# Another dealing of an adder layer's taps over three engines, and a first scan unit prepared by halves

## The chip, the cores and the metric

The kernel runs on one core of a Trainium2 chip. The metric is the device time of one execution in microseconds. Engines are named as in the profile: PE is TensorE, DVE is VectorE, ACT is ScalarE, POOL is GpSimd, SP issues the DMAs. PE is given a clock that can be throttled; the profile shows the share that was granted.

## The reference, cut to what matters

The program has four layers: an adder convolution, a Mamba block with three scan branches and a fusion, an attention with routed experts, and a deep linear-attention and spectral part. The change touches the first and the start of the second. After a group normalization of the input, with `x` as (8, 128, 16, 16), the first layer is

```python
def adder2d(x, W, stride, padding):           # W is (128, 128, 3, 3)
    ...
    out = -jnp.abs(W_col[:, :, None] - X_col[None, :, :]).sum(1)
```

Each of 128 filters takes nine taps of 128 channels, and sums the absolute differences over channels and taps. The result is added to `x`. The second layer normalizes over channels, projects to 256 channels `u`, and for each of the branches f, b and s does

```python
uc = jax.nn.silu(causal_conv1d(u, cw, cb))    # four taps
proj = uc @ xw.T                              # dt, Bm, Cm
delta = jax.nn.softplus(dt @ dw.T + db)
return selective_scan(uc, delta, -jnp.exp(A_log), Bm, Cm, D)
```

The scan has 16 states: h = exp(delta A) h + (delta u) B, and y sums h C over the states and adds u D.

## The kernel before

All data is fp32. Channels lie on the 128 partitions.

The first layer (`adder_layer`, L304) holds three copies of the padded image, shifted by 0, 1 and 2 columns; `tap(k)` is a view of one of them, 128 x 2048 (8 images of 256 pixels). Filters go in NG = 4 groups of FG = 32. For each filter and tap one engine makes a 128 x 2048 tile `d`, and PE adds it up over the channels (`add`, four matmuls of 512 columns with a selector of 32 columns, each on its own quarter of the columns of the array), all into one PSUM tile `o` of the group.

- Taps 1, 3, 5 (and 7, in some filters) are an absolute value on ACT (L421), with tiles of the tag da.
- Taps 0, 2, 4, 6, 8 (and 7 in the filters of MORE) are a maximum with the weight on DVE (L419), with tiles of the tag dv. By |w - x| = 2 max(w, x) - w - x, PE adds them with the selector 2, and the sums of weights and inputs are taken off by `wall` and `xsum`; MORE enters both.
- In the filters of JOIN, taps 0 and 2 are joined: the maximum of tap 0 is held, and one fused instruction on DVE (L413) makes max(tap 2, w) + held, in place. PE then has one tap less to add.

The pool of d has four buffers of each tag, so each producer can be four tiles ahead of PE. A planner may put instructions of an engine in another order than they are written in, by priorities; waits on buffers and data are its own. When a group is done, DVE adds `xsum` (L428), four DMAs on SP turn the result into `total` (L430), and DVE makes E.X from x, `wall` and `total`, by blocks of 512 (L434).

`x`, `total`, the shifted copies, the weights and the rest lie in one pool, l0, opened first. The pools of the second layer lie over it, and a tile there waits for the last access to what lay below.

The second layer's scans (`_scans`) treat units of (branch, pair of images), each a block of 512 columns and two halves of 128 channels. `first_unit` prepares the first of them with nothing beside it: centering on PE, square, Ln and Exp on ACT, the projection `pu` of each half, the convolution of each half as four matmuls with diagonal weights (eight passes of 512 columns, fp32 taking two), bias, sigmoid as Exp, Ln, Exp on ACT, the product `uc` on DVE, the projection `pp`, its copy `proj`, the DMA of its rows to DRAM, and softplus. Then `chunk` loads rows of B and C back, broadcast over partitions (bs and cs, two states to a load, SP queue); `decays` makes exp(delta A) in PSUM on ACT; `inputs` makes du x B (on DVE for the first state, on POOL for all others). The scan itself (L825) is on DVE, one per half and state, then the product with C (on POOL for states 1 and 8), then PE sums over the states. That loop is written in a fixed order by hand (`manual_schedule`), with the preparation of later units and the fusion in the gaps of it.

Of the kernel before, what the change touches and what calls it, by code (L numbers as in the profile page):

```python
# [10 lines left out]
F32 = mybir.dt.float32  # L11
AF = mybir.ActivationFunctionType
ALU = mybir.AluOpType
# [3 lines left out]
P = 128  # L17
B = 8
# [280 lines left out]
MORE = tuple(r for r in range(FG) if r % 5 in (0, 2))  # L299
JOINED = (0, 2)  # L300
JOIN = tuple(r for r in range(FG) if r % 5 in (1, 3))


def adder_layer(E):  # L304
# [8 lines left out]
    with ExitStack() as ctx:  # L313
        p = ctx.enter_context(tc.tile_pool(name="l0", bufs=1))
        accp = ctx.enter_context(tc.tile_pool(name="l0acc", bufs=3))
        absp = ctx.enter_context(tc.tile_pool(name="l0abs", bufs=4))
        po = ctx.enter_context(tc.tile_pool(name="l0po", bufs=2, space=PSUM))
        ps = ctx.enter_context(tc.tile_pool(name="l0ps", bufs=2, space=PSUM))

        x = p.tile([P, B, L], F32, tag="x", name="x0")  # L320
# [54 lines left out]
        def tap(k):  # L375
            kh, kw = divmod(k, 3)
            return shifted[kw][:, :, kh * 16 : kh * 16 + L]
# [26 lines left out]
        total = p.tile([P, NBLK, BLK], F32, tag="total", name="total")  # L404
        for g in range(NG):
            out = po.tile([P, BLK], F32, tag="o", name="o")
            for r in range(FG):
                f = g * FG + r
                maxima = MAX_TAPS + (MORE_TAPS if r in MORE else ())
                joined = JOINED if r in JOIN else ()  # L410
                for k in range(9):
                    if k in joined[1:]:
                        nc.vector.scalar_tensor_tensor(held, tap(k), w[:, k, f : f + 1], held, ALU.max, ALU.add)  # L413
                        add(out, sel2[:, FG - 1 - r : 2 * FG - 1 - r], held, False, False)
                        continue
                    d = absp.tile([P, B, L], F32, tag="dv" if k in maxima else "da", name="d")
                    wk = w[:, k, f : f + 1]
                    if k in maxima:
                        nc.vector.tensor_scalar(d, tap(k), wk, None, ALU.max)  # L419
                    else:  # L420
                        nc.scalar.activation(d, tap(k), AF.Abs, scale=-1.0, bias=wk)  # L421
                    if k in joined:
                        held = d
                        continue
                    sel = sel2 if k in maxima else sel1
                    row = slice(FG - 1 - r, 2 * FG - 1 - r)
                    add(out, sel[:, row], d, r == 0 and k == 0, r == FG - 1 and k == 8)
            nc.vector.tensor_add(sums[:, g, :], xsum, out)  # L428
            for i in range(NBLK):
                nc.sync.dma_start(total[g * FG : (g + 1) * FG, i, :], sums[i * FG : (i + 1) * FG, g, :])  # L430
# [71 lines left out]
def _scans(E, ctx, F):  # L502
# [116 lines left out]
    def softplus(k, s, h, proj, d, e, r, tag, gen):  # L619
# [7 lines left out]
        nc.scalar.activation(d, pd, AF.Relu, bias=db)  # L627
        yield LATER
        nc.scalar.activation(e, e, AF.Exp, scale=-1.0)
        one_e = ps.tile([P, UT], F32, tag=tag, name="one_e")  # L630
        nc.scalar.activation(one_e, e, AF.Identity, bias=E.ones[:, 0:1])
        yield LATER
        nc.vector.scalar_tensor_tensor(e, one_e, -1.0, e, ALU.add, ALU.subtract)
        nc.scalar.activation(r, one_e, AF.Ln)
        gen.tensor_sub(r, r, e)
# [10 lines left out]
    def prepare(k, s, p, got):  # L646
# [16 lines left out]
        for h in range(2):  # L663
            yield from softplus(k, s, h, proj, delta[:, h, :], pre[:, h, :], sig[:, h, :], "s", nc.gpsimd)
# [3 lines left out]
    def first_unit(k, s, p, got):  # L668
# [13 lines left out]
        us[p] = two.tile([P, 2, UT], F32, tag="u", name="u1")  # L682
        tags = ("f", "s")
        for h in range(2):
            pu = ps.tile([P, UT], F32, tag=tags[h], name="pu")
            E.mm(pu, E.w["in_proj"][:, h * P : (h + 1) * P], t)
            (nc.vector.tensor_copy if h else nc.scalar.copy)(us[p][:, h, :], pu)
# [5 lines left out]
        new, pre, sig, proj = tiles()  # L693
        uc, delta = new["uc"], new["delta"]
        for h in range(2):
            pc = ps.tile([P, UB, L], F32, tag=tags[h], name="pconv")
            for _ in convolution(k, s, h, us[p], pc):
                pass
            biased(s, h, pc, pre[:, h, :])
            for _ in sigmoid(sig[:, h, :], pre[:, h, :]):  # L700
                pass
            nc.vector.tensor_mul(uc[:, h, :], pre[:, h, :], sig[:, h, :])
        nc.scalar.copy(proj, projections(k, uc, proj, "f"))
        nc.sync.dma_start(new["rows"], proj[DTR:, :])
        parts = [
            softplus(k, s, h, proj, delta[:, h, :], pre[:, h, :], sig[:, h, :], tags[h], nc.vector) for h in range(2)
        ]
        for part in parts:
            next(part)
        for part in parts:  # L710
            for _ in part:
                pass
        nc.vector.tensor_mul(new["du"], delta, uc)  # L713
        got.update(new)
# [21 lines left out]
    def inputs(r, gen=nc.gpsimd):  # L736
        if r < states:
            dbs[r] = three.tile([P, 2, UT], F32, tag="db", name="dbu")
            gen.tensor_tensor(dbs[r], got[r // NST]["du"], bc(row("bs", r), 1, 2), ALU.mult)  # L739
# [52 lines left out]
    first_unit(*units[0], got[0])  # L792
# [3 lines left out]
    for g in range(3):  # L796
        decays(g)
    inputs(0, nc.vector)
# [1033 lines left out]
```

## Time and profile before

| | us |
|---|---|
| runs | 3077.44 median of 3, 3069.77 to 3080.7 |
| profiled execution, its own time | 3075.62 |
| its span | 3073.8 |
| PE busy | 2875.2 (94%) |
| DVE busy | 2451.8 (80%) |
| ACT busy | 2216.1 (72%) |
| first layer's taps on PE | 33.65 to 984.2 |
| last block of E.X done | 989.7 |
| first scan starts | 1023.64 |
| mean granted clock of PE | 0.988 |

A group's line gives the source line, engine and operation, the tiles written and read, the shape and the count; then the busy time and the mean duration of one in ns; then how long the engine was idle just before these instructions, and what ended the wait. A line of the timeline begins with the start and the length in us, and merges equal neighbours (xcount). A line of a window gives each engine's busy time in it, the granted clock, the share of the DMA engines and GB/s. PE's matmuls all have the line of a helper, L279, so their tiles tell them apart.

### The profile page before, as it was taken

Reading aid. Unit: us, or ns where it says so; the run is one execution under the profiler, and the core shown is the slowest. Engines: PE = TensorE matmul, PEld = TensorE weight load, DVE = VectorE, ACT = ScalarE, POOL = GpSimd, SP = SyncE. Lnnn points to the kernel's source line nnn. Section 1 sums busy time; section 2 is a strip of 40 time slices with the busy share of each in tenths; the row PEclk is TensorE's granted clock in tenths of the full one; section 3 lists DMA queues with packets and bytes.
Section 4 is the critical chain, followed back from the end, with each engine's and each line's share of the span. In section 5 each row is a group of like instructions: output and inputs, shape, how many; then the busy total and the mean of one; then the engine's idle time right before and its main releaser. Section 6 shows DMA issues by size and latency. Waiting matters only on the chain.

```text
span 3073.8 us, 42374 instructions
## 1 busy us (share of the span) xinstructions
PE 2875.2 (94%) x16602; PEld 1283.8 (42%) x16602; DVE 2451.8 (80%) x3452; ACT 2216.1 (72%) x2652; POOL 731.5 (24%) x445
## 2 busy tenths in 40 slices
PE   6999999999998788898898888999999999999999
PEld 2333333333332233443343444555555555654444
DVE  6999999999997799999999627887877777784331
ACT  6999999999997777778777324467778778777111
POOL 3000000000000599998999300000000000000110
PEclk9999999999999999999999999999999999999999
DMA  1000000000000444444344200000000000001100
GB/s 41 1 1 5 1 1 5 1 1 5 1 1 4 155 145 143 140 145 144 133 158 144 71 28 1 13 1 14 14 14 1 13 14 1 14 1 45 48 28 14
DMA packets 39197, 131.53 MB, mean 43 GB/s; under 512 B 7491, under 2 KB 10573, under 8 KB 37589
## 3 DMA queue, kind: packets, MB, share of 16 engines
q1 hardware_dynamic: 38564, 128.02, 11.9%
q8 instruction: 131, 2.15, 0.3%
q10 hardware_dynamic: 432, 0.79, 0.1%
q14 instruction: 70, 0.57, 0.1%
HBM read 125.91 MB, written 1.84 MB: 42 GB/s over the span
## 4 chain that ended last, share of the span: by engine, by line
PE 68%; DVE 16%; ACT 7%; POOL 5%; issue 3%; DMA 1%; DVEq 0%; ACTq 0%; POOLq 0%
PE o L279 31%; PE p L279 8%; DVE st L825 5%; PE acc L279 4%; PE g L279 4%; PE conv L279 3%; POOL dbu L739 2%; PE pc L279 2%; PE var L279 2%; PE pf L279 2%; PE pq L279 2%; PE po L279 1%; PE pn L279 1%; PE pconv L279 1%; PE pa L279 1%
## 5 line engine op out<-in xcount | busy, mean ns | idle before, releaser
L279 PE MATMUL o<-d,sel 128*32 128x512 f32 x8800 | 946.5, 592 | 5.5 <-DVE d L419 5.5
L421 ACT ACTIVATE d<-sh,w 128x2048 f32<-128x2048 f32 x460 | 886.2, 1996 | 64.0 <-PE o L279 54.4
L419 DVE TENSOR_SCALAR d<-sh,w 128x2048 f32<-128x2048 f32 x640 | 789.4, 1291 | 47.7 <-PE o L279 39.6
L739 POOL TENSOR_TENSOR dbu<-du,bs 128x1024 f32<-128x1024 f32 x191 | 446.9, 2365 | 994.8 <-DVE du L713 989.9
L279 PEld LDWEIGHTS o<-d,sel 128*32 128x32 f32 x8800 | 299.1, 110 | 652.1 <-issue 540.6
L825 DVE TENSOR_TENSOR_SCAN st<-da,dbu 128x512 f32<-128x512 f32 x384 | 446.1, 1206 | 17.6 <-POOL dbu L739 14.6
L279 PE MATMUL acc<-st,cst 128*128 128x512 f32 x768 | 369.4, 611 | 60.2 <-DVE st L836 59.9
L752 ACT ACTIVATE da<-delta,neg_a 128x510 f32<-128x510 f32 x384 | 256.9, 684 | 79.5 <-DVE st L825 78.1
L279 PEld LDWEIGHTS acc<-st,cst 128*128 128x128 f32 x768 | 142.2, 193 | 257.3 <-issue 139.5
L836 DVE TENSOR_TENSOR st<-st,pcs 128x1024 f32<-128x1024 f32 x168 | 205.2, 1222 | 17.9 <-ACT da L752 0.5
L1310 POOL TENSOR_TENSOR lw<-lw,turn 128x640 f32<-128x640 f32 x8 | 10.0, 1255 | 717.9 <-DVE turn L1309 626.6
L1087 ACT ACT_TABLE_LOAD x134 | 171.9, 1283 | 2.4
L1764 ACT COPY ug<-p 128x512 f32<-128x512 f32 x64 | 37.5, 585 | 180.4 <-PE p L279 180.4
L744 ACT COPY pcs<-cs 128x512 f32<-128x512 f32 x168 | 97.8, 582 | 55.8 <-DVE st L836 50.6
L279 PE MATMUL conv<-pad,f 128*128 128x512 f32 x288 | 133.1, 596 | 2.8 <-ACT pad L1001 2.3
L279 PE MATMUL p<-un,lw 128*128 128x512 f32 x256 | 123.6, 605 | 3.8 <-DVE un L1381 2.1
L413 DVE SCALAR_TENSOR_TENSOR d<-sh,w,d 128x2048 f32<-128x2048 f32 x52 | 122.3, 2352 | 1.9
L279 PE MATMUL p<-g,lw 128*128 128x512 f32 x256 | 116.4, 597 | 3.9 <-ACT g L1095 3.9
L279 PE MATMUL p<-T,H 128*128 128x512 f32 x256 | 113.8, 596 | 6.3 <-DVE ug L1766 5.3
L279 PE MATMUL g<-ug,me 128*128 128x512 f32 (+1 forms) x320 | 111.9, 509 | 0.0
L1095 ACT ACTIVATE ex<-ex 128x352 f32<-128x352 f32 x128 | 62.4, 494 | 52.2 <-DVE ex L1575 51.0
L279 PE MATMUL pf<-lw,rk 128*128 128x352 f32 x256 | 95.4, 470 | 0.3 <-DVE ek L1525 0.2
(347 smaller groups left out, 3946.2 us busy)
## 6 DMA issues: line engine op xcount, KB each, us to landing
bs<-rows SPq DMA_DIRECT2D x96, 512.0 KB, 3.7
cs<-rows SPq DMA_DIRECT2D x96, 512.0 KB, 4.6
m<-in_Mphi SPq DMA_DIRECT2D x8, 1024.0 KB, 4.8
lw<-in_layers SPq DMA_DIRECT2D x8, 948.0 KB, 4.7
f<-in_fuse SPq DMA_DIRECT2D x2, 1152.0 KB, 7.7
T<-in_T SPq DMA_DIRECT2D x1, 2064.0 KB, 7.8
x<-in_x SPq DMA_DIRECT2D x4, 256.0 KB, 7.1
total<-sums SPq DMA_DIRECT2D x16, 64.0 KB, 2.0
```

The source lines that it names most:

```text
L279: self.nc.tensor.matmul(out, lhsT=lhsT, rhs=rhs, start=start, stop=stop)
L413: nc.vector.scalar_tensor_tensor(held, tap(k), w[:, k, f : f + 1], held, ALU.max, ALU.add)
L419: nc.vector.tensor_scalar(d, tap(k), wk, None, ALU.max)
L421: nc.scalar.activation(d, tap(k), AF.Abs, scale=-1.0, bias=wk)
L739: gen.tensor_tensor(dbs[r], got[r // NST]["du"], bc(row("bs", r), 1, 2), ALU.mult)
L744: nc.scalar.copy(pcs[r], row("cs", r))
L752: nc.scalar.activation(das[g % 3][:, :, 1:], d[:, :, 1:], AF.Exp, scale=a)
L825: nc.vector.tensor_tensor_scan(st[:, h, :], da, dbs[r][:, h, :], 0.0, ALU.mult, ALU.add)
L836: nc.vector.tensor_tensor(st, st, bc(pcs[r][:, :], 1, 2), ALU.mult)
L1087: S.tc.keep_in_program_order(S.nc.scalar.preload_act_table_set(name))
L1095: S.nc.scalar.activation(out, src, func, **kw)
L1764: nc.scalar.copy(dst, p4)
```

## The change

In the first layer MORE is now 10 filters in 32 (r % 10 in 0, 3, 6; 13 before), and all other 22 are joined (13 before). In a joined filter the taps are written in the order 1, 0, 3, 2, 5, 4, 6, 7, 8. `x` and `total` have a pool of their own, opened after the others of the layer.

In `first_unit` both halves are projected first. Half 1's convolution is one scaling and three fused multiply-adds on DVE, straight from the projection in PSUM; its sigmoid is Exp on ACT, +1 and a reciprocal on DVE. Half 0 keeps PE and ACT. The copy of half 1's `u`, and the decay rates `neg_a`, are written behind the DMA of the rows. In softplus, for this unit alone, the Relu, the +1, and the last two sums are on DVE. The scan's first input is made by halves on POOL, and so the loads of bs and cs, the decays and these products stand between the halves.

```diff
-MORE = tuple(r for r in range(FG) if r % 5 in (0, 2))
+MORE = tuple(r for r in range(FG) if r % 10 in (0, 3, 6))
 JOINED = (0, 2)
-JOIN = tuple(r for r in range(FG) if r % 5 in (1, 3))
...
+        last = ctx.enter_context(tc.tile_pool(name="l0last", bufs=1))
...
-        x = p.tile([P, B, L], F32, tag="x", name="x0")
+        x = last.tile([P, B, L], F32, tag="x", name="x0")
...
-        total = p.tile([P, NBLK, BLK], F32, tag="total", name="total")
+        total = last.tile([P, NBLK, BLK], F32, tag="total", name="total")
...
-                joined = JOINED if r in JOIN else ()
-                for k in range(9):
+                joined = () if r in MORE else JOINED
+                order = (1, 0, 3, 2, 5, 4, 6, 7, 8) if joined else range(9)
+                for k in order:
+                    wk = w[:, k, f : f + 1]
                     if k in joined[1:]:
-                        nc.vector.scalar_tensor_tensor(held, tap(k), w[:, k, f : f + 1], held, ALU.max, ALU.add)
-                        add(out, sel2[:, FG - 1 - r : 2 * FG - 1 - r], held, False, False)
-                        continue
...
+                        d = held
+                        nc.vector.scalar_tensor_tensor(d, tap(k), wk, d, ALU.max, ALU.add)
...
@@ softplus
-        nc.scalar.activation(d, pd, AF.Relu, bias=db)
+        if alone:
+            nc.vector.tensor_scalar(d, pd, db, 0.0, ALU.add, ALU.max)
+        else:
+            nc.scalar.activation(d, pd, AF.Relu, bias=db)
         yield LATER
         nc.scalar.activation(e, e, AF.Exp, scale=-1.0)
...
+        if alone:
+            one_e = r
+            nc.vector.tensor_scalar_add(one_e, e, 1.0)
...
@@ first_unit
+        pus = [ps.tile([P, UT], F32, tag=t, name="pu") for t in tags]
         for h in range(2):
...
+            E.mm(pus[h], E.w["in_proj"][:, h * P : (h + 1) * P], t)
+        nc.scalar.copy(us[p][:, 0, :], pus[0])
+
+        u1, p1 = (a.rearrange("p (b l) -> p b l", l=L) for a in (pus[1], pre[:, 1, :]))
+        nc.vector.tensor_scalar(p1, u1, E.v("cw" + s, 7), E.v("cb" + s, 1), ALU.mult, ALU.add)
+        for m in range(1, 4):
+            o = p1[:, :, m:]
+            nc.vector.scalar_tensor_tensor(o, u1[:, :, : L - m], E.v("cw" + s, 7 - m), o, ALU.mult, ALU.add)
+        pc = ps.tile([P, UB, L], F32, tag="f", name="pconv")
+        for _ in convolution(k, s, 0, us[p], pc):
+            pass
+        t = sig[:, 1, :]
+        nc.scalar.activation(t, pre[:, 1, :], AF.Exp, scale=-1.0)
+        nc.vector.tensor_scalar_add(t, t, 1.0)
+        nc.vector.reciprocal(t, t)
+        nc.vector.tensor_mul(uc[:, 1, :], pre[:, 1, :], t)
+        biased(s, 0, pc, pre[:, 0, :])
+        for _ in sigmoid(sig[:, 0, :], pre[:, 0, :]):
+            pass
+        nc.vector.tensor_mul(uc[:, 0, :], pre[:, 0, :], sig[:, 0, :])
+        nc.scalar.copy(proj, projections(k, uc, proj, "f"))
+        nc.sync.dma_start(new["rows"], proj[DTR:, :])
+        got.update(new)
+        yield
+        nc.scalar.copy(us[p][:, 1, :], pus[1])
...
+        for h, part in enumerate(parts):
             for _ in part:
                 pass
-        nc.vector.tensor_mul(new["du"], delta, uc)
-        got.update(new)
+            nc.vector.tensor_mul(new["du"][:, h, :], delta[:, h, :], uc[:, h, :])
+            yield
...
-    first_unit(*units[0], got[0])
+    first = first_unit(*units[0], got[0])
+    next(first)
     for c in range(2):
         chunk("bs", 0, c)
         chunk("cs", NST, c)
-    for g in range(3):
-        decays(g)
-    inputs(0, nc.vector)
+    dbs[0] = three.tile([P, 2, UT], F32, tag="db", name="dbu")
+    for h in range(2):
+        next(first)
+        nc.gpsimd.tensor_mul(dbs[0][:, h, :], got[0]["du"][:, h, :], row("bs", 0))
+        decays(h)
+    decays(2)
     inputs(1)
     rows_of_c(0)
```

The planner's order around it: on DVE the half 0 product `uc` stands before half 1's, behind the reciprocal; PE does both `pp`, then the D term of half 0 (`acc`), then the two `pd` of softplus; the first scan stands on DVE before half 1's last sum and its `du`.

## The prediction, made before the changed kernel had run

> **What bounds the kernel now.** I began with the page's shares and its costliest groups. The first layer's three groups are the largest of their engines, and the fifth line here is its join:
>
> ```profile
> L279 PE MATMUL o<-d,sel 128*32 128x512 f32 x8800 | 946.5, 592 | 5.5 <-DVE d L419 5.5
> L421 ACT ACTIVATE d<-sh,w 128x2048 f32<-128x2048 f32 x460 | 886.2, 1996 | 64.0 <-PE o L279 54.4
> L419 DVE TENSOR_SCALAR d<-sh,w 128x2048 f32<-128x2048 f32 x640 | 789.4, 1291 | 47.7 <-PE o L279 39.6
> ...
> L413 DVE SCALAR_TENSOR_TENSOR d<-sh,w,d 128x2048 f32<-128x2048 f32 x52 | 122.3, 2352 | 1.9
> ```
>
> The idle column says who leads: TensorE waited 5.5 us in all (the start), while ScalarE (54.4) and VectorE (39.6) waited for TensorE to give buffers back. So this third of the span is TensorE's: 1100 taps (8 records each) in 946.5 us, 0.8605 us a tap. The timeline gives the start-to-start intervals, which a mean of durations hides:
>
> ```profile
> 938.37 2.35 DVE L413 SCALAR_TENSOR_TENSOR d<-sh,w,d 128x2048 f32<-128x2048 f32 x1
> ...
> 940.64 10.85 DVE L419 TENSOR_SCALAR d<-sh,w 128x2048 f32<-128x2048 f32 x9
> ...
> 941.40 13.52 ACT L421 ACTIVATE d<-sh,w 128x2048 f32<-128x2048 f32 x7 [1.07 <-PE o L279]
> ...
> 951.64 1.29 DVE L419 TENSOR_SCALAR d<-sh,w 128x2048 f32<-128x2048 f32 x1
> ...
> 952.96 2.35 DVE L413 SCALAR_TENSOR_TENSOR d<-sh,w,d 128x2048 f32<-128x2048 f32 x1
> ```
>
> A maximum follows a maximum after (10.85-1.29)/8 = 1.195 us; the join starts 952.96-951.64 = 1.32 after the maximum that it needs; 940.64-938.37 = 2.27 after a join comes the next. An absolute value takes (13.52-2.00)/6 = 1.92.
>
> Then the timeline between the layers, where one chain runs at a time:
>
> ```profile
> 989.75 0.35 ACT L689 ACTIVATE neg_a<-vecs 128x32 f32<-128x32 f32 x2 [11.22 <-DVE X L434]
> 990.01 0.58 ACT L674 ACTIVATE ln_rstd<-xc 128x512 f32<-128x512 f32 x1
> ...
> 1002.91 0.69 ACT L603 ACTIVATE pre<-pconv,vecs 128x512 f32<-128x512 f32 x1 [4.74 <-PE pconv L279]
> ...
> 1009.12 0.69 DVE L702 TENSOR_TENSOR uc<-pre,sig 128x512 f32<-128x512 f32 x1 [2.72 <-ACT sig L611]
> ...
> 1013.06 0.69 ACT L626 ACTIVATE pre<-pd,vecs 128x512 f32<-128x512 f32 x1 [1.53 <-PE pd L279]
> ...
> 1023.64 2.34 DVE L825 TENSOR_TENSOR_SCAN st<-da,dbu 128x512 f32<-128x512 f32 x2
> ...
> 1027.15 4.56 DVE L825 TENSOR_TENSOR_SCAN st<-da,dbu 128x512 f32<-128x512 f32 x4
> ```
>
> With zero at the start of the xc matmul (987.70), the second half's uc begins at 21.4, softplus at 25.4, the first scan at 35.9 and state 1's at 39.45. From there VectorE repeats with no gap, so a shift of state 1 shifts everything after it.
>
> **Part 1, the dealing.** Per group of 32 filters 22 are joined (13 before) and 10 move tap 7 to VectorE (13). Over 128 filters: joins 52 -> 88, maxima 640 -> 592, absolute values 460 -> 472, taps on TensorE 1100 -> 1064.
> - TensorE: 1064 x 0.8605 = 915.6, 31 us less.
> - ScalarE: 472 x 1.92 = 906.
> - VectorE: 592 x 1.195 + 88 x 2.27 = 707 + 200; in the changed order 52 joins stand right behind the maximum that they need, and pay 1.32-1.195 more: 6.5. Together 914 (the same sum before: 890).
>
> Three nearly equal queues, where TensorE led by 50 us. VectorE's fifth tap starts at 40.79 in the trace (the start before it does not change). From there VectorE has 914 - 4 x 1.195 = 909, three group sums inside at 0.6 (2 us) and the first filter's stalls as now (2 us): done at 953.8. The lag of TensorE behind VectorE's last tap stays 984.19-981.22 = 2.97. That makes 956.8, if VectorE never waits for a buffer. How often does it? In the trace a buffer is usable 1.11 to 1.17 us after its tap's first matmul, and data is used 0.05 us after it is made. I carried the three queues through both orders tap by tap with these intervals and four buffers for each producer. For before this gives ScalarE 53 us of waits and VectorE 39 (trace: 54.4 and 39.6). For after it gives VectorE 6 us of buffer waits and TensorE some 35 short waits of 0.25 us. So 963 instead of 984.2: **-21 us**. With no wait at all it is -27; with the release 0.15 us later, or 15 us of waits, -13.
>
> The tap order (1,0,3,2,...) lets TensorE begin a joined filter with ScalarE's tap; it adds no work. Three memsets fewer on GpSimd at the start lie before its wait for a load: nothing.
>
> **Part 2, x and total in a pool of their own.** neg_a lay over x, so ScalarE waited for the last X (989.72), and the Square behind it in the queue, ready at 988.9, started at 990.01. Now neg_a waits only for the last taps: **-1.1 us**. What is late next is the matmul itself.
>
> **Part 3, halves.** Each step at its trace duration, zero as above.
> - pu starts at 6.7 (now 7.8), its halves are out at 8.7 and 10.4; eight warm passes of convolution for half 0 until 14.05, as the trace has them after the first half.
> - Removed from TensorE: eight passes of 0.43 (3.4 us). Added to VectorE for half 1: one tensor-scalar and three fused steps out of PSUM, 0.69 + 3 x 0.72: done at 13.35. ScalarE Exp 0.63, VectorE +1 0.55 (row L681): 14.6. Then the reciprocal of 128x512, for which there are only small rows:
>
> ```profile
> L361 DVE RECIPROCAL rs<-rs 128x8 f32<-128x8 f32 x1 | 0.2, 203 | 4.4 <-ACT rs L357 4.4
> ...
> L941 DVE RECIPROCAL sm<-sm 128x2 f32<-128x2 f32 x8 | 1.3, 158 | 0.0
> ```
>
> Six elements more cost 45 ns: 7.5 ns each, so 512 cost 3.9 us. The other end is [...]as in the multiply: 0.69. [...]I take 3.9, done at 18.5.
> - Half 0 on ScalarE: bias, copy of u1 (0.5, new in between), Exp, Ln, Exp, so uc 0 could start at 14.05+3.35 = 17.4. It is queued behind the reciprocal: 18.55; uc 1 at 19.2. With 0.69 it would be 17.4, and the sum 1.15 lower.
> - pp 0 starts at 19.3 (the last one at 22.2 now).
>
> Here the clock speaks. TensorE now stays at work beside half 0's sigmoid; afterwards it idles from 14 to 19.3.
>
> ```profile
> 997.00:999.00 2.00, 2.00 (x3) 0.65 (x2) 0.00 (x0) 0.58 (x1) 0.00 (x0) 0.50 0.00 0
> 1001.00:1003.00 2.00, 2.00 (x6) 0.94 (x5) 0.00 (x0) 0.09 (x1) 0.00 (x0) 1.00 0.00 0
> ```
>
> The third figure from the end is the granted clock; at 0.50 passes follow each other after 0.855 us, at 1.00 after 0.43. [...] By the row of now (pp at full clock) the four pp passes end at 21.2 and softplus begins at 22.9. [...]they run at half: pp until 22.95, acc half 0 until 24.4, pd after that[...]: softplus at 25.6, against 25.4 now. [...]
> - Softplus to state 1, by the new order. From its start t: Relu, +1, and the subtractions alternate on VectorE with Exp and Ln on ScalarE; delta 0 at t+5.8, du 0 at 6.5, GpSimd's half product (1.26, row L635's shape) until 7.8, scan 0 of state 0 at 7.85. This is a new wait: behind that scan on VectorE stand the add and the du of half 1, though ready at 7.1, and GpSimd's second product waits for that du. So add and du until 10.4, product until 11.7, scan 11.75, C product until 14.2; GpSimd's state 1 product (2.35, behind both halves in its queue) until 14.1. State 1 scans at t+14.25, against 1027.15-1013.06 = 14.1 now. The first scan comes 2.7 us earlier relative to softplus, and gives it back one state on.
> - On SP the rows store and its four loads keep their order; the first bs goes out 1.7 us after the store, as now, at about t-0.3; GpSimd needs it at t+6.5 and such loads land in about 3.7 (row of issues): hidden, 3 us spare. If late, it costs its lateness once.
>
> State 1: 25.6+14.25 = 39.85 against 39.45: **+0.4 us**. Full clock all along and a short reciprocal: -3.5. Half clock also in the convolution[...]: +2.5.
>
> **Sum.** 3073.8 - 21 + 0.4 = 3053.2 span. Outside the span lie 3075.62-3073.8 = 1.8, and the median shown is 1.8 above the profiled time: **3057**.
>
> **Rivals.**
> 1. The queues hold each other up: 15 to 20 us of buffer waits rather than 6. For: averages within 1.5% on three engines and only four buffers. Against: a joined or unjoined filter costs VectorE the same 7.2 us, so its load doesn't swing. Time: 3066.
> 2. All works: VectorE never waits, TensorE keeps its clock. -27-3 = 3047. Against: the gap of 5 us.
> 3. Slower: ScalarE waits 1.07 us once per joined filter (52 times, all of its 54 us). If that were a price of joining rather than slack, ScalarE would need 906 + 88 x 1.07 = 1000, 56 above TensorE's 944: 3130. It decides from 0.45 us a join. Against: TensorE never waits for ScalarE in the trace.
> 4. The dealing gains nothing: buffer waits of 27 us or more on VectorE: 3077. Against: it waits 39 us now only because TensorE is 50 us longer.
>
> **Numbers.** Likeliest 0.74 (its own range 3049 to 3064); rival 1 0.13; rival 2 0.09; rivals 3 and 4 0.02 each. Runs of before differ by 11 us (3069.8 to 3080.7), and 0.3%, about 9 us, is what tells from no change: below 3068.2. Range 3046 to 3068: from rival 2 to rival 1's middle. Faster 0.91, same 0.07 (rival 4 and the slower part of rival 1), slower 0.02.
>
> **What would show it.** Rows of the layer: VectorE's idle for TensorE under 15 us, TensorE idle near 10 with VectorE named, X some 21 us earlier. neg_a before the Square with no wait for X. Reciprocal near 3.9 us, uc 0 directly behind it. Clock 0.50 at pp. Scan of half 1 about 3.9 us behind half 0's. Wrong would be: ScalarE or TensorE still leading the layer, or a state 1 more than 4 us from its place behind X.

## The result, and the profile after

The changed kernel takes 3056.92 us (median, 3054.22 to 3062.77); the kernel before, beside it, 3076.87. The ratio is 0.9941, with a 95% interval of 0.9928 to 0.9954. The profiled execution took 3055.99 us with a span of 3054.2. The forecast was 3057; that the median meets it to 0.1 us is chance, since single executions lie up to 6 us away from it. One execution in the tables below, of the kernel with 124 units joined, took 3705.6 us at a granted clock of 0.748; it is left out of that kernel's median and ratio.

The first layer's groups on the page after:

```profile
L279 PE MATMUL o<-d,sel 128*32 128x512 f32 x8512 | 922.8, 593 | 7.5 <-DVE d L421 5.5
L423 ACT ACTIVATE d<-sh,w 128x2048 f32<-128x2048 f32 x472 | 899.6, 1994 | 29.8 <-PE o L279 23.2
L421 DVE TENSOR_SCALAR d<-sh,w 128x2048 f32<-128x2048 f32 x592 | 724.3, 1290 | 12.5 <-PE o L279 9.4
...
L417 DVE SCALAR_TENSOR_TENSOR d<-sh,w,d 128x2048 f32<-128x2048 f32 x88 | 206.7, 2349 | 1.9
```

The idle column has changed sides. VectorE waits 9.4 us for buffers where it waited 39.6, ScalarE 23.2 where it waited 54.4. TensorE's busy time fell by 24 us though its taps fell by 31 us' worth: a stretched tap counts as busy. From start to start, 36 of the 1064 taps take more than the usual 0.86 us, 33 of them about 1.07 and three 1.43: 8.6 us that before did not have. Each of the 36 starts 0.05 or 0.06 us after an instruction of VectorE has ended, so it is VectorE's tiles that TensorE waits for. The last tap ends at 962.62 us instead of 984.19.

The timeline of the changed kernel between the layers (start and length in us; brackets hold the idle time before and its releaser):

```profile
959.75 0.35 ACT L724 ACTIVATE neg_a<-vecs 128x32 f32<-128x32 f32 x2 [1.72 <-issue]
...
966.14 2.08 PE L279 MATMUL xc<-X,center 128*128 128x512 f32 x2 [3.52 <-DVE X L436]
...
973.76 3.75 PE L279 MATMUL pu<-xn,w_in_proj 128*128 128x512 f32 x4 [2.79 <-issue]
...
981.87 3.35 DVE L712 RECIPROCAL sig<-sig 128x512 f32<-128x512 f32 x1
...
985.14 0.63 DVE L717 TENSOR_TENSOR uc<-pre,sig 128x512 f32<-128x512 f32 x1
...
985.82 3.43 PE L279 MATMUL pp<-uc,w_xproj 128*40 128x512 f32 x4 [3.97 <-DVE uc L717]
...
991.52 0.69 ACT L628 ACTIVATE pre<-pd,vecs 128x512 f32<-128x512 f32 x1 [1.66 <-PE pd L279]
...
998.07 1.26 POOL L824 TENSOR_TENSOR dbu<-du,bs 128x512 f32<-128x512 f32 x1 [965.56 <-DVE du L737]
...
999.36 1.22 DVE L853 TENSOR_TENSOR_SCAN st<-da,dbu 128x512 f32<-128x512 f32 x1 [1.18 <-POOL dbu L824]
...
1003.27 1.22 DVE L853 TENSOR_TENSOR_SCAN st<-da,dbu 128x512 f32<-128x512 f32 x1 [1.38 <-POOL dbu L824]
...
1005.66 3.44 DVE L853 TENSOR_TENSOR_SCAN st<-da,dbu 128x512 f32<-128x512 f32 x3
```

State 1's first scan, the third scan of the kernel, stands 43.04 us behind the last tap (42.96 before) and 39.52 behind xc (39.45 before). So the shift at state 1 is -21.5 us, all of it from the first layer. From there to the end before took 2046.65 us and after 2048.54: 1.9 us went back, and the span is 19.6 us shorter.

The same stretch by windows (busy time of PE, PEld, DVE, ACT and POOL; the third figure from the end is the granted clock):

```profile
965.60:979.20 13.60, 9.59 (x11) 3.35 (x12) 5.58 (x10) 2.62 (x5) 0.00 (x0) 0.50 0.04 10
979.30:986.00 6.70, 2.73 (x7) 0.93 (x7) 5.93 (x6) 3.67 (x6) 0.00 (x0) 1.00 0.00 0
986.10:989.40 3.30, 3.30 (x5) 0.61 (x4) 0.26 (x1) 0.12 (x1) 0.00 (x0) 0.50 0.00 0
```

The half clock covers xc, var and both pu, ends 1.9 us into the 4.5 us of the convolution, and comes back for pp. In the kernel before it had set in one matmul later: var and pu had the same lengths, but xc ran at the full clock, and so in the forecast.

```profile
987.70 1.12 PE L279 MATMUL xc<-X,center 128*128 128x512 f32 x2 [3.51 <-DVE X L434]
990.64 2.07 PE L279 MATMUL var<-ln_rstd,mean 128*128 128x512 f32 x2 [1.82 <-ACT ln_rstd L674]
995.51 3.75 PE L279 MATMUL pu<-xn,w_in_proj 128*128 128x512 f32 x4 [2.79 <-issue]
```

### The profile page after: what moved, and what is told of

It is laid out like the page before. It is cut to its first block, busy times and chain, and to the rows that moved or that the text cites. A ratio compares the mean times of both kernels' runs of the same rounds, so it can differ in the third digit from the quotient of the medians.

```text
span 3054.2 us, 41648 instructions
## 1 busy us (share of the span) xinstructions
PE 2859.8 (94%) x16306; PEld 1260.9 (41%) x16306; DVE 2469.8 (81%) x3449; ACT 2226.4 (73%) x2658; POOL 733.0 (24%) x444
## 4 chain that ended last, share of the span: by engine, by line
PE 67%; DVE 17%; ACT 7%; POOL 5%; issue 3%; DMA 1%; DVEq 0%; ACTq 0%; POOLq 0%
PE o L279 30%; PE p L279 8%; DVE st L853 5%; PE acc L279 5%; PE g L279 4%; PE conv L279 3%; POOL dbu L763 2%; PE pc L279 2%; PE var L279 2%; PE pf L279 2%; PE pq L279 2%; PE pa L279 1%; PE po L279 1%; PE pn L279 1%; PE px L1610 1%
## 5 line engine op out<-in xcount | busy, mean ns | idle before, releaser
L279 PE MATMUL o<-d,sel 128*32 128x512 f32 x8512 | 922.8, 593 | 7.5 <-DVE d L421 5.5
L423 ACT ACTIVATE d<-sh,w 128x2048 f32<-128x2048 f32 x472 | 899.6, 1994 | 29.8 <-PE o L279 23.2
L421 DVE TENSOR_SCALAR d<-sh,w 128x2048 f32<-128x2048 f32 x592 | 724.3, 1290 | 12.5 <-PE o L279 9.4
L279 PEld LDWEIGHTS o<-d,sel 128*32 128x32 f32 x8512 | 273.9, 110 | 655.6 <-issue 533.6
L279 PE MATMUL acc<-st,cst 128*128 128x512 f32 x768 | 382.2, 631 | 59.0 <-DVE st L864 58.6
L417 DVE SCALAR_TENSOR_TENSOR d<-sh,w,d 128x2048 f32<-128x2048 f32 x88 | 206.7, 2349 | 1.9
```

The costliest lines, as they stand in the source:

```text
L279: self.nc.tensor.matmul(out, lhsT=lhsT, rhs=rhs, start=start, stop=stop)
L417: nc.vector.scalar_tensor_tensor(d, tap(k), wk, d, ALU.max, ALU.add)
```

## The experiments

Each kernel below the second row was run beside the kernel before, in three sets of runs in which before's medians were 3078.20, 3078.01 and 3079.33 us. Rows of different sets are compared by their ratios and by the marks in the trace, not by their medians. "Last tap", "transition" (last tap to the third scan) and "rest" (from there to the end) are from each one's profiled execution.

| kernel | median us | ratio to before, 95% | last tap | transition | rest |
|---|---|---|---|---|---|
| before | 3076.87 | | 984.19 | 42.96 | 2046.65 |
| changed | 3056.92 | 0.9941, 0.9928 to 0.9954 | 962.62 | 43.04 | 2048.54 |
| dealing alone | 3054.04 | 0.9937, 0.9919 to 0.9955 | 962.73 | 43.85 | 2045.12 |
| dealing and pool | 3047.80 | 0.9923, 0.9896 to 0.9950 | 963.93 | 42.12 | 2039.55 |
| pool and halves | 3081.42 | 1.0016, 1.0007 to 1.0025 | 984.69 | 41.96 | 2055.65 |
| taps 0 to 8 | 3092.62 | 1.0063, 1.0043 to 1.0082 | 996.71 | 41.99 | 2045.50 |
| taps 0 to 8, 5 buffers | 3046.02 | 0.9894, 0.9874 to 0.9913 | 951.78 | 41.87 | 2048.55 |
| 5 buffers | 3046.22 | 0.9899, 0.9880 to 0.9919 | 953.05 | 42.93 | 2040.52 |
| 124 units joined | 3094.61 | 1.0063, 1.0041 to 1.0085 | 997.63 | 43.05 | 2049.22 |
| extra matmuls | 3055.44 | 0.9930, 0.9911 to 0.9949 | 962.15 | 37.76 | 2046.59 |
| both halves first | 3058.82 | 0.9944, 0.9924 to 0.9964 | 964.08 | 43.31 | 2044.81 |
| old unit, 5 buffers | 3045.56 | 0.9887, 0.9871 to 0.9904 | 953.30 | 43.08 | 2048.52 |
| extra matmuls, 5 buffers | 3041.23 | 0.9878, 0.9863 to 0.9893 | 952.19 | 37.75 | 2051.86 |
| old unit, extra, 5 buffers | 3043.28 | 0.9885, 0.9871 to 0.9900 | 953.01 | 39.67 | 2051.12 |

### One part at a time

The dealing alone, on the kernel before:

```diff
+MORE = tuple(r for r in range(FG) if r % 10 in (0, 3, 6))
...
+                joined = () if r in MORE else JOINED
+                order = (1, 0, 3, 2, 5, 4, 6, 7, 8) if joined else range(9)
```

> The kernel before with the new dealing of the first layer alone (which units are joined, and the order of taps 0 to 3); no pool of its own for x and total, and the first scan unit as it was. Theory (the dealing shortens the longest queue, VectorE's): the o taps end at 963 us instead of 984.2, the first state scan stands 35.9 us and the third 39.4 us after the xc matmul as before, and the whole is 20 to 21 us shorter than before, 3056 to 3057 us: all or more of what the whole change brought. Rival (the new first unit carries a part of the gain): the whole is less than 17 us shorter, over 3060 us.

The last tap ends at 962.73 us, and the ratio is that of the whole change within the intervals. The dealing carries the gain; the rival falls (the median is 2 us below the range of the theory). The third scan comes 40.33 us after xc, 0.9 later than expected; the mean granted clock of its transition was 0.77, against 0.80 in the kernel before.

The dealing and the pool, the first unit as before:

```diff
+        last = ctx.enter_context(tc.tile_pool(name="l0last", bufs=1))
...
-        x = p.tile([P, B, L], F32, tag="x", name="x0")
+        x = last.tile([P, B, L], F32, tag="x", name="x0")
...
-        total = p.tile([P, NBLK, BLK], F32, tag="total", name="total")
+        total = last.tile([P, NBLK, BLK], F32, tag="total", name="total")
```

> The changed kernel less its third part: the new dealing and the own pool for x and total, with the first scan unit prepared as before. Theory (the halves are worth +0.1 to +0.4 us): the time is within 1.5 us of the changed kernel's 3056.9, and the third scan is 38.3 to 39.5 us after xc. Rival (the halves pay): 3 us or more above the changed kernel.

The transition is 42.12 us, 1.7 below the dealing alone and 0.9 below the changed kernel; the third scan comes 38.59 us after xc, within the theory's range. Part of both differences is the clock: in this execution the clock was 1.00 from 977.90 us on, ahead of the convolution, which took 6.99 us and the two pu 3.36, where the dealing alone has 7.85 and 3.75. The same old unit in "old unit, 5 buffers", whose transition had a mean granted clock of 0.76 where this one has 0.80, takes 43.08. (The expectation gives the halves +0.1 to +0.4; the prediction's own steps give them +1.5, since its +0.4 has the pool's -1.1 in it.) The median is 9 us below the changed kernel's, against the theory, though the intervals of the two ratios overlap. At the third scan its span is 0.4 us behind the changed kernel's (1006.05 against 1005.66); the 9 us lie in the rest, 2039.55 against 2048.54, where the two programs issue the same instructions in the same order. Its runs also spread over 17 us (3044.39 to 3061.15). Whether that rest belongs to the old unit is asked again below.

The pool and the halves, without the dealing:

```diff
-MORE = tuple(r for r in range(FG) if r % 10 in (0, 3, 6))
+MORE = tuple(r for r in range(FG) if r % 5 in (0, 2))
+JOIN = tuple(r for r in range(FG) if r % 5 in (1, 3))
...
-                joined = () if r in MORE else JOINED
-                order = (1, 0, 3, 2, 5, 4, 6, 7, 8) if joined else range(9)
+                joined = JOINED if r in JOIN else ()
```

> The kernel before with the own pool for x and total and the new first unit by halves; the dealing of the first layer stays. Theory (these two parts nearly cancel: 1.1 us less from the pool, 0.1 to 0.4 us more from the halves): the o taps end at 984 us as before, the third scan is within 1 us of 39.5 us after xc, and the time is within 2 us of 3076.9. Rival A (two matrix-engine queues and three helpers shorten the preparation by a few us, but the dealing hides it): the third scan 3 us or more sooner than 39.4 after xc, and 3 to 5 us less in all. Rival B: the 3.35 us reciprocal and the scan of half 0 ahead of half 1's add cost more than the pool gives: 2 us or more slower.

The third scan stands at 984.69 + 41.96 = 1026.65, 0.5 us sooner than before, and 38.44 after xc, just outside the theory's 1 us around 39.5, on the early side. The end is 3 to 5 us later (medians and ratio), as rival B said, but not by what rival B named: the reciprocal and the scan order lie ahead of the third scan. The rest took 2055.65, 9 us more than before. This is the scan stage of this kernel:

```profile
1026.65:1735.21 708.56, 633.27 (x1488) 270.96 (x1489) 659.79 (x593) 528.94 (x873) 635.37 (x307) 0.96 0.42 146
```

and this the same stage before:

```profile
1027.15:1729.50 702.35, 618.23 (x1492) 263.93 (x1493) 659.36 (x593) 529.03 (x873) 633.94 (x307) 0.99 0.42 148
```

The mean granted clock is 0.96 against 0.99, TensorE's busy time for the same matmuls grew by 15 us, and the stage by 6. So the later stages' time goes with the clock that they get. Over 89 executions of all these kernels, with each kernel's own mean taken out, 0.001 less mean clock goes with 1.5 us more time, and the scatter falls from 3.3 to 2.4 us. By that slope, as an estimate, the mean clocks of "pool and halves" and of before (0.983 and 0.986) are worth 5 us, and those of the changed kernel and of "dealing and pool" (0.984 and 0.988) 6 us. This is a correlation; why one kernel gets more of the clock in its later stages than another is not shown.

### The order of the taps

The joined units' taps in the order 0 to 8 again:

```diff
-                order = (1, 0, 3, 2, 5, 4, 6, 7, 8) if joined else range(9)
+                order = range(9)
```

> The changed kernel with the taps of a joined unit in the order 0 to 8 again instead of 1, 0, 3, 2. Theory (only the amount of work in the longest queue counts): the o taps end within 1.5 us of 962.6 and the time is within 2 us of 3056.9. Rival (the order keeps the joined pair's two operations of VectorE apart and TensorE fed): more and longer waits of TensorE for VectorE's d, the o taps 4 us or more later, over 3061 us.

The theory fell, by far: the same work on each engine, 34 us longer and slower than before the change. Its groups:

```profile
L279 PE MATMUL o<-d,sel 128*32 128x512 f32 x8512 | 925.2, 593 | 38.1 <-DVE d L417 32.6
L423 ACT ACTIVATE d<-sh,w 128x2048 f32<-128x2048 f32 x472 | 906.0, 1994 | 54.9 <-PE o L279 46.3
L421 DVE TENSOR_SCALAR d<-sh,w 128x2048 f32<-128x2048 f32 x592 | 731.9, 1291 | 39.8 <-PE o L279 33.6
```

The timeline of VectorE alone, for two joined units:

```profile
439.76 3.67 DVE L421 TENSOR_SCALAR d<-sh,w 128x2048 f32<-128x2048 f32 x3
443.35 2.35 DVE L417 SCALAR_TENSOR_TENSOR d<-sh,w,d 128x2048 f32<-128x2048 f32 x1
445.61 6.06 DVE L421 TENSOR_SCALAR d<-sh,w 128x2048 f32<-128x2048 f32 x5
452.03 3.86 DVE L421 TENSOR_SCALAR d<-sh,w 128x2048 f32<-128x2048 f32 x3 [0.36 <-PE o L279]
456.32 1.29 DVE L421 TENSOR_SCALAR d<-sh,w 128x2048 f32<-128x2048 f32 x1 [0.43 <-PE o L279]
457.65 2.35 DVE L417 SCALAR_TENSOR_TENSOR d<-sh,w,d 128x2048 f32<-128x2048 f32 x1
```

and of TensorE alone, in the same stretch:

```profile
439.53 5.33 PE L279 MATMUL o<-d,sel 128*32 128x512 f32 x48
445.75 21.67 PE L279 MATMUL o<-d,sel 128*32 128x512 f32 x200 [0.88 <-DVE d L417]
468.29 1.92 PE L279 MATMUL o<-d,sel 128*32 128x512 f32 x16 [0.88 <-DVE d L417]
```

All three engines wait for one another. In the old order a joined unit gives TensorE one tap of ScalarE's and then asks for the tap that costs VectorE a maximum and a join, 1.3 + 2.3 us. VectorE can only have that ready if it ran ahead, and just before, it was held for want of a buffer (0.36, 0.43). With 50 us of slack under TensorE this cost nothing; with three equal queues each such pause is lost. TensorE pauses 36 times, mostly for 0.88 us: the 32.6 us of the first row, and nearly all of the 34.

Does the order itself cost it, or the four buffers? Both edits together:

```diff
-        absp = ctx.enter_context(tc.tile_pool(name="l0abs", bufs=4))
+        absp = ctx.enter_context(tc.tile_pool(name="l0abs", bufs=5))
...
-                order = (1, 0, 3, 2, 5, 4, 6, 7, 8) if joined else range(9)
+                order = range(9)
```

> The changed kernel with both edits: taps of a joined unit in the order 0 to 8, and five buffers of d for each engine. Theory (with the old order VectorE's two operations for one tap leave TensorE without a tap, and with four buffers VectorE cannot have run ahead for it: the 34 us of the order are the queues' hold on each other): the fifth buffer takes most of the 34 us away, and the o taps end at 953 to 970 us, against 996.7 with four. Rival (the old order costs a pause of TensorE at each joined unit whatever the buffers): the o taps end at 983 to 990 us, the 9.6 us of the fifth buffer below 996.7.

The last tap ends at 951.78 us, 45 us sooner than with four buffers and a little below the theory's range (two executions). The rival falls: the order is worth 34 us with four buffers and nothing with five.

### The fifth buffer and the joins

```diff
-        absp = ctx.enter_context(tc.tile_pool(name="l0abs", bufs=4))
+        absp = ctx.enter_context(tc.tile_pool(name="l0abs", bufs=5))
```

> The changed kernel with five buffers of d for each of the two engines in place of four. Theory (VectorE's queue has no slack left: 592 max operations, 88 fused ones, 931 us busy to the last o tap, with 9.4 us of waits for a buffer): a further buffer lets VectorE run those 9.4 us ahead and TensorE's 37 short waits go with them, so the o taps end 4 to 9 us earlier, at 953 to 959 us, and the whole is 4 to 9 us shorter. Rival (VectorE's waits are the consequence of being ahead early in a group and behind at its end, so that work alone sets the layer): the o taps within 2 us of 962.6.

```profile
L279 PE MATMUL o<-d,sel 128*32 128x512 f32 x8512 | 916.1, 592 | 3.5 <-DVE d L421 3.2
L423 ACT ACTIVATE d<-sh,w 128x2048 f32<-128x2048 f32 x472 | 898.0, 1993 | 21.7 <-PE o L279 15.0
L421 DVE TENSOR_SCALAR d<-sh,w 128x2048 f32<-128x2048 f32 x592 | 719.9, 1286 | 7.6 <-PE o L279 4.1
```

9.6 us in the layer, and a ratio of 0.9899 where the changed kernel has 0.9941, with intervals that do not meet. 7.8 of the 9.6 are TensorE's long intervals (8.6 to 0.8 us). The start gives 1.1: TensorE's first tap begins 2.3 us sooner (31.31 for 33.64), but its second only 1.1 (39.47 for 40.55). TensorE is now 916.1 us busy and 3.5 idle: the layer is again bounded by its taps. So in the changed kernel no one queue's work set the layer, but how far nearly equal ones could run ahead.

All but four units joined:

```diff
-MORE = tuple(r for r in range(FG) if r % 10 in (0, 3, 6))
+MORE = (31,)
```

> The changed kernel with 124 of the 128 units joined instead of 88 (one unit in 32 keeps tap 7 on VectorE): ScalarE has 508 operations d instead of 472, TensorE 1028 taps instead of 1064. Theory (the longest queue sets the layer): ScalarE's 508 operations at 1.906 us are 968 us instead of 900, VectorE's work falls a little and TensorE's by 31 us, and the o taps end near 1005 us (968 and the 37 us or so before ScalarE's first d), 43 us later than with 88, and 21 later than before the change: 3097 to 3102 us. Rival (TensorE sets the layer, fewer taps are better): the o taps end 20 to 31 us earlier, near 935 us, and the whole at 3027 to 3037 us.

```profile
L423 ACT ACTIVATE d<-sh,w 128x2048 f32<-128x2048 f32 x508 | 962.8, 2000 | 6.7 <-POOL sh L371 6.4
L279 PE MATMUL o<-d,sel 128*32 128x512 f32 x8224 | 925.0, 595 | 36.0 <-ACT d L423 33.7
```

ScalarE is busy 962.8 us and waits for no buffer; TensorE waits 33.7 us for it. The last tap ends at 997.63, 7 us before the estimate, and the median is 2 us below the theory's range: the lead-in to ScalarE's first d is 28.2 us, not the 37 it assumed. The longest queue sets the layer, and a join costs ScalarE no wait of its own.

### The clock of the transition

Ten further 128x512 matmuls, into a tile that nothing reads:

```diff
+    def keep_warm(n):
+        t = ps.tile([P, UT], F32, tag="cs", name="warm")
+        for _ in range(n):
+            E.mm(t, ident, E.cst[:, 0:UT])
...
+        keep_warm(3)
         pxc = ps.tile([P, UT], F32, tag="s", name="xc1")
...
         E.mm(var, E.mean, rstd)
+        keep_warm(3)
...
         for _ in convolution(k, s, 0, us[p], pc):
             pass
+        keep_warm(4)
...
-    next(first)
+    with tc.manual_schedule(engines={nc.tensor.engine}):
+        next(first)
```

(The last lines keep TensorE's instructions in the order as written; in the trace the matmuls that do work stand in the order of the changed kernel.)

> The changed kernel with ten further 128x512 matmuls into a PSUM tile that nothing reads: three ahead of the xc matmul, three behind the var matmul, four behind the first unit's convolution. They change no output; the order of TensorE's instructions is else kept. Theory (the transition's matmuls run at the half clock because TensorE is idle for most of it): the granted clock stays at 1.00 through the transition (0.77 in the changed kernel), xc, var, the two in-projections, the convolution and the projection take about half their time (1.1 to 1.8 us less each, less what the extra ones put in front of them), and the third state scan comes 3 to 6 us sooner after the last o tap than the changed kernel's 43.04 us. Rival A (the extra matmuls delay as much as the clock saves): within 1 us of 43.04. Rival B (the clock that the scan stage gets hangs on this window too): the scan stage, 702.3 us at a mean clock of 0.97, gets 3 us or more shorter besides.

```profile
962.20:988.50 26.30, 22.37 (x48) 7.94 (x48) 15.03 (x23) 9.66 (x19) 0.00 (x0) 1.00 0.10 30
```

The granted clock is 1.00 from the last tap to beyond pd. The transition takes 37.76 us, 5.3 less, and the third scan stands 34.24 us after xc instead of 39.52; xc takes 1.12 us instead of 2.08, pu 1.96 instead of 3.75, pp 1.91 instead of 3.43. So keeping the granted clock at 1.00 up to 988.5 us was worth 5.3 us in this stretch, the time of the extra matmuls already paid. Rival A falls. Rival B finds little: the scan stage is 1.1 us shorter (701.19). The whole kernel is no shorter beyond the noise: its ratio, 0.9930, lies inside the interval of the changed kernel's. With five buffers the two gains were to add up:

> The changed kernel with five buffers of d and the ten extra matmuls in the transition. Theory (the two gains lie in different stages and add up): the o taps at 953 us, the transition 37.8 us as with the extra matmuls alone, 14 to 15 us less than the changed kernel at the third scan, and 3041 to 3043 us in all. Rival (what the transition gains is given back in the clock of later stages): over 3044 us.

They do at the third scan (952.19 + 37.75 = 989.94, 15.7 us before the changed kernel's). The median, 3041.23, is the lowest of the study and in the theory's range. But against five buffers alone the gain is not clear of the noise: the ratios, 0.9878 and 0.9899, have intervals that overlap, and between the two profiled executions the rest differs by 11 us the other way (2051.86 and 2040.52).

### The old first unit again

The changed kernel less its third part, with five buffers, and then with ten extra matmuls too:

> The changed kernel less its third part (the first scan unit as before), with five buffers of d. Theory (the halves bring no gain: the third scan stood 42.12 us after the last o tap without them and 43.04 with them): the o taps at 953 us, the transition 42 to 43.5 us, the whole at or below that of the halves with five buffers, 3046.2: 3037 to 3046 us. Rival (the 9 us by which the kernel without halves was shorter in four runs were chance): within 2 us of 3046.

> The changed kernel less its third part, with five buffers of d and ten extra matmuls at the same places (three ahead of xc, three behind var, four behind the first unit's convolution, here both halves of it). Theory (at the full clock the old preparation gains less than the halves do, since TensorE had more to do in it and was at 0.80 rather than 0.77): the transition 38 to 40 us, against 37.8 with the halves, and the whole 3035 to 3042 us. Rival (the old preparation is the shorter one at either clock): a transition below 37.5 us.

With five buffers the old unit and the halves are alike, 3045.56 and 3046.22, with transitions of 43.08 and 42.93 us; the rests of the profiled executions differ by 8 us the other way round (2048.52 and 2040.52). The number also fits the theory ("at or below 3046.2"), but no gain is left for it, so the rival holds: the 9 us of "dealing and pool" are not a property of the old unit. With the extra matmuls (mean granted clocks of 0.97 with the halves and 0.91 with the old unit) the halves are ahead by 1.9 us (37.75 against 39.67), as that theory said, though the whole, 3043.28, is above its range. About 0.6 of the 1.9 belongs to where the extra matmuls stand: in the old unit four of them lie ahead of pp, and from the second half's uc to the copy of pp it takes 1.79 us where "dealing and pool" takes 1.15. That the rest comes from TensorE having less to do is argued, not shown.

### VectorE's order at the first scan

```diff
-        for part in parts:
-            next(part)
-        for part in parts:
-            next(part)
-            next(part)
+        yield
+        for _ in range(5):
+            for part in parts:
+                next(part)
...
+        for _ in first:
+            pass
+        dbs[0] = three.tile([P, 2, UT], F32, tag="db", name="dbu")
+        for h in range(2):
+            nc.gpsimd.tensor_mul(dbs[0][:, h, :], got[0]["du"][:, h, :], row("bs", 0))
+            decays(h)
```

(inside the block whose order is as written; a pause of softplus stands before its last two sums, and the next unit's convolution is moved behind these lines).

> The changed kernel with VectorE's order at the end of the first unit written out: the add and the du of both halves, and GpSimd's two products, stand before the first state scan, as the second half's stood behind the scan of half 0. Theory (the first scan in front of half 1's add is a new wait that the halves brought: the scan of half 1 came 3.9 us behind that of half 0): both scans of state 0 stand back to back, and the third scan comes about 2.6 us sooner after xc, 36.9 us instead of 39.5. Rival (GpSimd's second product or ScalarE's decays set that scan in any case): the third scan within 0.7 us of 39.5.

```profile
991.10 3.77 PE L279 MATMUL pd<-proj,w_dtproj 8*128 8x512 f32 x4 [0.67 <-ACT proj L720]
...
994.91 0.69 ACT L628 ACTIVATE pre<-pd,vecs 128x512 f32<-128x512 f32 x1 [1.02 <-PE pd L279]
...
1001.01 1.26 POOL L833 TENSOR_TENSOR dbu<-du,bs 128x512 f32<-128x512 f32 x1 [967.85 <-DVE du L738]
1001.17 1.65 DVE L648 TENSOR_TENSOR delta<-delta,sig 128x512 f32<-128x512 f32 x1
...
1002.86 0.69 DVE L738 TENSOR_TENSOR du<-delta,uc 128x512 f32<-128x512 f32 x1
1003.47 1.22 DVE L856 TENSOR_TENSOR_SCAN st<-da,dbu 128x512 f32<-128x512 f32 x1
...
1004.93 1.22 DVE L856 TENSOR_TENSOR_SCAN st<-da,dbu 128x512 f32<-128x512 f32 x1 [0.25 <-POOL dbu L833]
```

xc started at 967.60, so half 1's scan stands 37.33 us behind it (37.13 in the changed kernel), and the third scan 39.79: the theory's 36.9 falls, and the number is within the rival's range. The scans are 1.46 us apart instead of 3.91, but because half 0's came later. Taking the halves in turn puts du of half 0 1.5 us back (32.24 after xc, 30.75 in the changed kernel), and half 1's sum takes 1.65 us where it took 0.67. It starts 0.16 us after GpSimd's product and ends 0.55 after that one's end. In the changed kernel the sum began at 1000.50 us, when GpSimd was free (its products ran from 998.07 to 999.33 and from 1001.97).

The order is not all that differs, however. Here the half clock lasted through pd:

```profile
984.80:1001.90 17.10, 12.87 (x15) 4.12 (x16) 9.36 (x14) 5.46 (x9) 0.89 (x1) 0.50 0.38 127
```

In the changed kernel it had ended by 989.5, and pd took 1.98 us where it takes 3.77 here; ScalarE waits 1.02 us for its second half. The D term of half 0, ahead of pd in the changed kernel, stands behind it here. By the two lengths of pd, an estimate, 1.8 us of the 39.79 are the clock's. At an equal clock the third scan would then come near 38.0: sooner than 39.52, still not at 36.9. So this run does not show that the place of the first scan costs nothing.

## Why the prediction was right, point by point

**The dealing, -21 us: right.** The last tap moved by -21.57, and the dealing alone gives it. VectorE's last tap ended at 959.66 us (963 less the lag of 2.97 makes 960.0). Its buffer waits were 9.4 us (6 expected), of which 3.71 lie ahead of the fifth tap, where the sum begins; TensorE's short waits were 36 (35 expected). The bound without waits, 956.8 (-27), was mis-sized: five buffers reach 953.05, because the first filter's stalls, taken as given, shrink too, and TensorE then sets the end. That the sum runs along VectorE's queue alone also says too much: with four buffers VectorE and TensorE wait for each other in turn, and no wait of TensorE is for ScalarE.

**The tap order, "it adds no work": the step that the sum rests on without saying so.** The order was in the tap-by-tap reckoning but was not priced. With four buffers it is worth 34 us: without it this dealing is 14 us slower than before. Rival 1 (the queues hold each other up) names the mechanism that then rules; it lost because of the order, not because the load doesn't swing.

**The pool, -1.1 us: right as to the wait, about half as to its worth.** neg_a begins at 959.75 without waiting for X. But with xc at the half clock (2.08 us in the changed kernel, 1.98 in "dealing and pool", 1.12 before) the Square would not have been ready at 1.2 us behind xc: it began at 2.57 without the pool (dealing alone) and at 2.02 with it ("dealing and pool"). Of the 1.7 us between these two transitions 0.5 are thus the pool's; the rest is the clock in pu and in the convolution, as said above.

**The halves, +0.4 with the pool: right in the sum (39.52, expected 39.85), by errors that cancel.** xc ran at the half clock (2.08 us for 1.12), which the forecast did not have: pu began at 7.62 behind xc, not 6.7. In the other direction, the reciprocal took 3.35 us, not 3.9, and from pp to softplus it was 5.7 us, not 6.3. uc 0 stood behind the reciprocal as expected (19.0, expected 18.55); pp began at 19.68 (19.3) at the half clock, softplus at 25.38 (25.6). From softplus to half 1's scan 11.75 us were forecast and 11.75 measured, to state 1 14.25 and 14.14. "Pool and halves" shows the forecast with pu where it assumed it, at 6.68: pp at 18.74, softplus at 24.32 and state 1 at 38.44. So the steps up to softplus were 1.3 us too long, and the half clock on xc hid it. That state 1 came out within 0.4 us is luck.

Half rate at pp was the right choice over the row of before, which had pp at the full clock: with it softplus was to begin at 25.6, by the row at 22.9, and it began at 25.38. No trace of before showed that pp would get half rate and pd full rate again; it was an assumption of the author's. In the changed kernel the granted clock was 0.50 from 965.59 to 979.24 us, from xc on, and from 986.07 to 989.48, in pp. In the 3.41 us ahead of these two drops TensorE was busy for 0.44 and 0.25 us: xc came behind a nearly idle stretch just as pp did. The forecast took another course of the clock into account only for the convolution, as an outer case. The experiments show both ends: the same new unit reaches state 1 at 38.35 to 38.47 after xc in three kernels, 39.42 to 39.55 in three others, and 34.23 and 34.24 with the extra matmuls.

**"The first scan comes 2.7 us earlier and gives it back": right.** It came at 33.22 instead of 35.94, and state 1 was where it had been. The reason given, that the add and the du of half 1 stand behind the first scan "though ready at 7.1", is neither confirmed nor refuted: the run that moved the scan away came 0.3 us later, but with pd at the half clock (3.77 us for 1.98) and with its add, beside GpSimd's product, at 1.65 us for 0.67.

**The sum.** The span was forecast at 3053.2 and is 3054.2. The missing term is the rest, +1.9 us, which the forecast set at zero since VectorE "repeats with no gap". The scan stage did repeat (702.35 and 702.32). The loss lies behind it, in a stretch that went from 926.80 us (1904.50 to 2831.30) to 929.70 (1881.30 to 2811.00), with TensorE busy for 888.43 and 890.95 us and at the half clock for 10.2 and 15.9; what is left got 1.0 shorter. At 2039.6 to 2055.7 over these kernels, the rest is a term of several us that differs from run to run. What fixes it is not settled here, and why "pool and halves" had the lowest clock and the longest rest stays open.

**The rivals.** 1 fell at four buffers and this order. 2 needed the fifth buffer, which alone gives its 3047 (3046.22 us); with the clock kept up as well it is 3041. 3 is refuted by 124 joins without a buffer wait on ScalarE; 4 by the dealing alone.

## What to carry to other kernels

When a change balances engines that were unequal, the slack that hid the order of work and the depth of the buffers is gone: price both again, by asking which tap an engine has to hand while another does its double work. Here one more buffer was worth half as much as the whole change, and the tap order more than it. In a chain of single small steps between two busy stages, a few matmuls that nothing needs kept the clock up (a mean of 0.94, 0.77 without them) and took 5.3 us off the chain, though no gain of the whole kernel stands clear of the noise here. And judge a part by the marks inside its stage, and look at the clock before reading them: a whole-kernel difference of 9 us between two kernels was gone when the comparison was made again with one more buffer in each.

## What the runs showed of the hardware that was not expected

- A reciprocal of 128x512 on VectorE took 3.35 us, 6.5 ns an element, in the changed kernel, in "both halves first" and in "extra matmuls". The forecast's 3.9 us was an estimate from the two small rows of before, at 7.5 ns an element.
- In "both halves first" a VectorE sum of two SBUF tiles that started 0.16 us after a GpSimd product of two SBUF tiles took 1.65 us instead of 0.67, and ended 0.55 us after the product. In the kernel before it is the other way round: a GpSimd product that starts 0.10 us after VectorE's (1022.42 and 1022.32) takes 3.33 us instead of 2.35. VectorE's product with a PSUM operand took its usual 1.22 us beside GpSimd (at 1031.82, with GpSimd's product of 1030.34 to 1032.69 under way). In both slow cases it was the instruction that started second that took longer; what held it up is not shown.
- The half clock came in stretches of 3.413 us or of two to four times that (but for the last one of each trace), also within the scan stage, where TensorE was 88% busy over the whole (618 of 702 us): five of them in that stage before (20 us) and eleven after (44 us), for the same instructions. In "pool and halves" the stage's mean of 0.96 makes it about 57 us, an estimate. The mean hides what came before each: in the 3.4 us ahead of each of these 16 drops TensorE was busy for 6 to 50% of the time. In each of these two traces (before and changed) all drops lie on one grid of 3.413 us. They cost that stage little: it took 700.6 to 704.5 us in twelve of the fourteen kernels, 706.1 and 708.6 in two, with VectorE busy for 657.5 to 659.8 us in all of them.
